# A transformer block in fp32 on one core: product 1 of a two-level Strassen scheme becomes a joint product too, and the sum it shares with products 6 and 7 is added to x by GpSimd

## The chip, the cores and the metric

The kernel runs on one core of a Trainium2 chip. The core has five engines with a queue of instructions each: TensorE (PE in the profile) multiplies matrices into PSUM, VectorE (DVE) and ScalarE (ACT) read PSUM and do elementwise work, GpSimd (POOL) does elementwise work on SBUF, and SyncE (SP) starts the DMAs. Each works its queue off in order; semaphores make an instruction wait for one of another engine. The metric is the device time of one execution in microseconds.

## The reference

x is 8 batches of 1024 rows of 1024 columns, fp32. Two steps follow each other, each added to x:

```python
x = x + xattn(layernorm(x), ctx, mask)        # 64 context rows a batch
x = x + ffn(layernorm(x), weight, lora_A, lora_B, router_w)

# xattn: softmax over the 64 unmasked rows of  h @ ctx.T / 32,  then  @ ctx
# ffn, h = layernorm(x):
base   = h @ weight.T                          # 1024 x 1024
probs  = softmax(h @ router_w.T)               # 8 experts; the top 2, weights made to sum to 1
Ax     = h @ lora_A.T                          # 8 experts x rank 16 = 128 columns
out    = base + 2 * sum over experts of  w_dense[e] * Ax[e] @ lora_B[e].T
```

## The kernel before, in words

**Pairs and rounds.** A tile has 128 rows of x; a pair has two tiles (r = 0, 1), 32 pairs in all (NP). `first()` (L896) takes the first two pairs and builds the weight sums. After it `quad(u)` (L1093) runs 15 times, for u = 2, 4, ..., 30: a round. It computes the ffn of the pairs u and v = u+1, and beside it the attention of the pairs behind them, called n, m, f and g (u+2 to u+5).

**The order is written out by hand.** All five engines run under `tc.manual_schedule` (L1307): every engine takes its instructions in the order in which the Python calls issue them. Semaphores come from the buffers: a write to a tile waits for its former readers. `hooks` are calls that `joint` makes at a given step, so that work of other pairs is issued between blocks of matmuls.

**The base product in two levels of Strassen's scheme (Winograd's form).** Level 1 halves the two tiles, the 1024 inputs and the 1024 outputs of a pair. That gives 7 products of 128x512 by 512x512, with sums of the operands: `has[u][:, 0]`, `has[u][:, 1]`, `hbs`, s1, s2, s4 (`rt_sums` L629 and `rt_sum_3` L640 form them on GpSimd), and of the weights: w11, w21, w22, t1 to t4. Product 8 here is the low-rank part of one quarter (`lora`, L694). Level 2 pairs the pairs u and v: `joint` (L788) does one product for both in 7 blocks of two 256-wide matmuls instead of 8. Its operand sums come from `joint_sums` (L774, four GpSimd operations), its weight sums q1 to q4 from `quarter_sums` (L680). Products 2 to 7 are joint. Product 1 is plain (`product`, L710): four 512-wide matmuls a pair, added to three quarters of x by `one_add` (L735) on VectorE. Each partial sum of a joint product goes from PSUM into x by VectorE (`to_x`, L806). Product 6 belongs to three quarters: it goes into the tile's own spent operand (`t_of`, L740), its first parts by ScalarE and VectorE copies, and GpSimd's `six_add` (L744) adds that to x. Product 7 belongs to two quarters and is added to x twice by VectorE.

**Routing.** `rt_low_rank_tile` (L572) multiplies a tile with the 128 low-rank columns and 8 router columns into `pa`, a PSUM tile of one bank (L574). ScalarE copies it to `axl`, a tile of one buffer (L582, L583). `rt_top` (L585) finds the two best experts on VectorE, with one exponential on ScalarE in the middle (L595), and scales `axl` in place (L612). `rt_turn_low_rank` (L614) transposes it on TensorE (`trw`, L621) and ScalarE copies the result to `axwt` (L623), which all `lora` matmuls read.

**Attention and norms.** `x_sums`, `x_squares` and `x_root` (L189 to L212) give the first norm on ScalarE; a pass over a tile is an ACTIVATE of 1024 columns. `att_scores` (`sct`), `att_sc` (`sc`), `att_shift`, `att_exp`, `att_divide`, `att_turn_p` (`ptp`), `att_readout` (`ro`) and `att_add` follow. `f_sums`, `f_squares`, `f_std`, `f_rows` give the second norm; its rows go to DRAM and come back blocked, and VectorE transposes them (`rt_turn_tile`). `att_turn_tile` does the same with x.

**PSUM.** Six banks (`ps_pp`) go round among chains, joint products (`jl`, `ju`), read-outs and the like; one bank each is kept for the attention and for the router.

**The start of a round (L1104 to L1224).** TensorE's order for u = 4 to 26: product 1 of u, the end of the joint product 4 before, the low-rank products of u, product 1 of v with `sc` inside, the low-rank products of v with `trw` of u between its tiles, product 8 of u, read-out of n, `ptp`, scores of f and g, read-out of m, then joint 6, 2, 7, 3, 5, 4. `rt_top(u)` is issued ahead of the second tile's x_sums and of x_squares.

Of the kernel before, what the change touches and what calls it, by code (L numbers as in the profile page):

```python
# [24 lines left out]
def kernel(  # L25
# [631 lines left out]
    quarters = {}  # L657
# [4 lines left out]
    def quarter_sums_steps(name: str, w):  # L662

        by = nc.gpsimd.tensor_tensor
        b11, b12, b21, b22 = [quarter(w, i, j) for i in (0, 1) for j in (0, 1)]
        q2, q3, q4 = [
            const.tile([P, HK, HH], F32, name=f"{name}_{i}") for i in (2, 3, 4)
        ]
        quarters[name] = b11, b21, b22, b12, q2, q3, q4

        def one():
            by(q3, b22, b12, ALU.subtract)

        def two():
            by(q2, q3, b11, ALU.add)
            by(q4, b21, q2, ALU.subtract)

        return one, two

    def quarter_sums(name: str, w):  # L680
        for do in quarter_sums_steps(name, w):
            do()

# [51 lines left out]
    def one_add(u: int, which=(0, 1, 2)):  # L735

        for i in which:
            add(u, pps[u][1], *((0, 0), (0, 1), (1, 0))[i])
# [5 lines left out]
    def six_add(u: int):  # L744
        for r, c in ((1, 0), (1, 1), (0, 1)):
            xc = xts[u][r][:, ts(c, HB)]
            nc.gpsimd.tensor_tensor(xc, xc, t_of(u), ALU.add)  # L747
# [3 lines left out]
    BOTH = {5: ((0, 1), (1, 1)), 7: ((1, 0), (1, 1))}  # L751
# [12 lines left out]
    def operand(i: int, p: int):  # L764
# [5 lines left out]
        return {3: sms[p][:, 1], 5: sms[p][:, 0], 7: has[p][:, 1]}[i]  # L770
# [17 lines left out]
    def joint(i: int, u: int, hooks, final: bool = False, aside: bool = False):  # L788
# [12 lines left out]
        name = {2: "w21", 3: "w22", 4: "t4", 5: "t1", 6: "t2", 7: "t3"}[i]  # L801
# [4 lines left out]
        def to_x(p, src, first: int, n: int):  # L806
            if i == 6:
                t = t_of(p)[:, first : first + n]
                if n == HH and (p == u and first == 0 or aside):
                    nc.scalar.copy(t, src)  # L810
                elif n == HH:
# [84 lines left out]
    def first():  # L896
# [153 lines left out]
        t1_two()  # L1050
        quarter_sum("t2")
# [7 lines left out]
        quarter_sums("w21", w21)  # L1059
        product_add(1, 7)  # L1060
# [15 lines left out]
        quarter_sums("w22", w22)  # L1076
        quarter_sum("w22")
        quarter_sum("w21")
        quarter_sums("t4", t4)
        att_scores(4)  # L1080

        def last():
            end()
            store(1, 1)
            quarter_sum("t4")
# [5 lines left out]
    pending = []  # L1091

    def quad(u: int):  # L1093
# [10 lines left out]
        product(u, 1, (lambda: att_sc(n)) if early else None, 1)  # L1104
# [4 lines left out]
        if new_mem:  # L1109
            mask_bias(b)  # L1110
        pending.pop()()
        if early:
            att_divide(n)
        one_add(u)
        rt_low_rank_tile(u, 0)
        if early:
            att_turn_p(n)
        rt_low_rank_tile(u, 1)
        if early:
            att_turn(m)  # L1120
        rt_turn_tile(v, 0)
        rt_top(u)
        rt_turn_tile(v, 1)
        if late:
# [4 lines left out]
            product(v, 1, lambda: att_sc(m))  # L1129
            if far:  # L1130
                att_turn_tile(f, 0)
                load_xs(g, (1,))
                att_turn_tile(f, 1)
            att_rstd(m)
            att_shift(m)
        rt_sum_3(u)
        rt_sums(v)
        if early:
            load_xs(f)
        elif far:  # L1140
            load_xt(f)
        if late:
            rt_low_rank_tile(v, 0)
            rt_turn_low_rank(u, bank_of(f"trw_{u}")[:, : 2 * P])
            att_exp(m)
            one_add(v, (0,))
        elif early:
            att_readout(n)
            att_scores(m)
            load_xs(g, (0,))  # L1150
            product(
                v, 1,
                {0: lambda: att_sc(m), 1: lambda: rt_turn_low_rank(u), 2: lambda: product(u, 8)},
            )
            att_rstd(m)
            att_exp(m)
            att_add(n)
            att_divide(m)
            f_sums(n)
# [3 lines left out]
            rt_low_rank_tile(v, 0)  # L1163
            att_turn_tile(f, 1)
        else:
            product(v, 1)
            rt_low_rank_tile(v, 0)
            rt_turn_low_rank(u, bank_of(f"trw_{u}")[:, : 2 * P])
        if far:
            att_turn_tile(g, 0)  # L1170
        if late:
            att_divide(m)
        if far:
            att_turn_tile(g, 1)
        if late and not far:
            att_readout(n)
            att_add(n)
        rt_low_rank_tile(v, 1)
        if early or late and not far:
            att_turn_p(m, True)  # L1180
        if not early:
            product(u, 8)
        joint_sums(6, u)
        rt_sum_3(v)
        if late and far:
            att_readout(n)
            att_turn_p(m, True)
        product_add(u, 8)
        if late and far:
# [6 lines left out]
        if far or not more:  # L1196
            rt_top(v)
        if more:
            att_readout(m)
        if late and not far:  # L1200
            att_add_tile(m, 0)
            rt_top(v)
        if late:
# [3 lines left out]
        if late and not far:  # L1207
            att_add_tile(m, 1)
        elif more:
            att_add(m)  # L1210
        left_over = []
        if late:
            one_add(v, (1,))
            left_over.append(lambda: one_add(v, (2,)))
        else:
            one_add(v)

        hooks = {5: left_over, 7: []}
        hooks[5 if more else 7].append(lambda: rt_turn_low_rank(v))
        if more:  # L1220
            hooks[2] = [lambda: f_squares(n), lambda: f_std(n)]
        if next_mem:
            hooks[5].append(lambda: turn_mem((f + 2) // PPB))
        end_6 = joint(6, u, hooks, aside=not more)  # L1224
        joint_sums(2, u)

        def low_v():
            product(v, 8)
            product_add(v, 8)

        def six():
            end_6()
            for p in (u, v):
                six_add(p)

# [119 lines left out]
```

## Time and profile before

| what | value |
| --- | --- |
| median of 3 runs | 1103.91 us (1103.2 to 1103.92) |
| span of the profiled execution | 1101.5 us |
| median less that span | 2.4 us |
| POOL, DVE, ACT busy in the span | 567.1, 819.8, 556.2 us |
| DMA moved | 174.01 MB, mean 158 GB/s |
| table loads of ACT, each | 1.28 us (four a round) |

The page gives the span, from the first to the last instruction; the time of a run holds a little more around it. An engine's busy time is the time in which its instructions ran. In the page's second part the span is cut in 40 slices; every slice but the first and the last has PE at 90% or more, and the granted clock at its full value. A timeline line is: start, length, engine, source line, operation, tile written <- tiles read, shape, number of records merged. An fp32 matmul leaves two records. What stands in brackets is the idle time before it and who ended it.

### The profile page before, as it was taken

How to read it: one execution, taken by the hardware profiler on the slowest of the kernel's cores; microseconds unless marked ns; L12 is line 12 of the kernel's file. 1: busy time of each engine (PE TensorE's matmuls, PEld its weight loads, DVE VectorE, ACT ScalarE, POOL GpSimd, SP SyncE). 2: the span in 40 equal slices, each digit the busy share in tenths (PEclk: the TensorE clock that was granted, in tenths of full speed). 3: DMA queues.
4: the chain of work that ended last, by engine and by line, in shares of the span. 5: the costliest groups of instructions: out<-in, count | busy, mean ns of one | idle time of the engine just before them, and what ended most of it. 6: DMA issues, size and time to landing. Idle time of an engine off the chain costs nothing.

```text
span 1101.5 us, 17562 instructions
## 1 busy us (share of the span) xinstructions
PE 1090.6 (99%) x5864; PEld 846.6 (77%) x5864; DVE 819.8 (74%) x2069; ACT 556.2 (50%) x1063; POOL 567.1 (51%) x629
## 2 busy tenths in 40 slices
PE   8999999999999999999999999999999999999998
PEld 6555787887878788787787878878787787877877
DVE  6666977769777687867869778687777778667665
ACT  4577363727539173573726638174472735636010
POOL 0079563635647265373644646356372644647372
PEclk9999999999999999999999999999999999999999
DMA  9857446363474625646265473635636355432301
GB/s 229 212 181 218 137 154 217 100 200 125 153 230 131 211 82 193 197 148 199 101 196 152 153 230 100 195 118 190 203 135 193 108 203 147 153 115 91 139 1 77
DMA packets 104921, 174.01 MB, mean 158 GB/s; under 512 B 12928, under 2 KB 77440, under 8 KB 104832
## 3 DMA queue, kind: packets, MB, share of 16 engines
q1 hardware_dynamic: 104832, 172.90, 50.3%
q8 instruction: 47, 0.77, 0.3%
q14 instruction: 42, 0.34, 0.1%
HBM read 107.84 MB, written 65.01 MB: 157 GB/s over the span
## 4 chain that ended last, share of the span: by engine, by line
PE 95%; DVE 2%; POOL 1%; ACT 1%; DMA 1%; SPq 0%; issue 0%; DVEq 0%; ACTq 0%; POOLq 0%
PE jl L703 28%; PE ju L703 21%; PE pa L578 10%; PE ch L703 9%; PE ro L480 5%; PE sct L412 5%; PE ju L695 4%; PE jl L695 3%; PE plain L703 3%; PE ch L695 2%; PE j L703 1%; DVE xT L89 1%; PE trw L621 1%; DMA xs<-in_x_dram 1%; PE ptp L466 1%; SPq L83 0%
## 5 line engine op out<-in xcount | busy, mean ns | idle before, releaser
L818 DVE TENSOR_TENSOR xt<-jl,xt 128x256 f32<-128x256 f32 x421 | 191.6, 485 | 139.6 <-PE jl L703 90.8
L818 DVE TENSOR_TENSOR xt<-ju,xt 128x256 f32<-128x256 f32 (+1 forms) x210 | 110.7, 551 | 56.2 <-PE ju L703 52.6
L635 POOL TENSOR_TENSOR s<-hA,hB 128x512 f32<-128x512 f32 x31 | 39.7, 1280 | 208.4 <-PE jl L703 92.9
L747 POOL TENSOR_TENSOR xt<-xt,hA 128x512 f32<-128x512 f32 x90 | 111.4, 1275 | 29.1 <-DVE hA L814 29.1
L195 ACT ACTIVATE junk<-xt 128x1024 uint8<-128x1024 f32 x60 | 63.2, 1053 | 123.6 <-DMA xt<-in_x_dram 123.1
L703 PE MATMUL ch<-w,hA 128*128 128x512 f32 x248 | 113.7, 593 | 0.0
L642 POOL TENSOR_TENSOR hA<-hA 128x512 f32<-128x512 f32 x31 | 39.6, 1277 | 139.8 <-PE pa L578 139.8
L703 PE MATMUL ju<-w,s_j 128*128 128x256 f32 x360 | 94.7, 385 | 0.2
L703 PE MATMUL ju<-t,s_j 128*128 128x256 f32 x360 | 92.7, 380 | 1.4 <-ACT hA L810 0.9
L692 DVE TENSOR_TENSOR xt<-ch,xt 128x512 f32<-128x512 f32 x124 | 81.3, 678 | 9.6 <-PE ch L703 4.5
L296 ACT ACTIVATE h<-xt,of_f 128x1024 f32<-128x1024 f32 x60 | 71.2, 1232 | 22.9 <-DVE of_f L292 14.1
L692 DVE TENSOR_TENSOR xt<-ro,xt 128x512 f32<-128x512 f32 x128 | 79.6, 676 | 3.7 <-PE ro L480 3.7
L703 PEld LDWEIGHTS ju<-t,s_j 128*128 128x128 f32 x360 | 66.2, 190 | 18.1 <-issue 5.3
L703 PEld LDWEIGHTS ch<-w,hA 128*128 128x128 f32 x248 | 44.7, 190 | 42.7 <-issue 41.8
L703 PE MATMUL jl<-t,s 128*128 128x256 f32 x300 | 76.0, 384 | 0.0
L703 PEld LDWEIGHTS ju<-w,s_j 128*128 128x128 f32 x360 | 63.9, 190 | 15.7 <-issue 6.8
L89 DVE STREAM_TRANSPOSE xT<-xs 128x1024 f32<-128x1024 f32 x60 | 73.6, 1229 | 0.6
L578 PEld LDWEIGHTS pa<-art_sb,hA 128*128 128x128 f32 x512 | 66.3, 190 | 9.8 <-issue 8.6
L578 PE MATMUL pa<-art_sb,hA 128*128 128x136 f32 x512 | 70.0, 280 | 0.0
L204 ACT ACTIVATE junk<-xt,of_x 128x1024 uint8<-128x1024 f32 x60 | 68.9, 1149 | 2.0
L578 PE MATMUL pa<-art_sb,hB 128*128 128x136 f32 x512 | 69.8, 279 | 0.0
L253 ACT ACTIVATE junk<-xt,of_f 128x1024 uint8<-128x1024 f32 x60 | 69.0, 1149 | 1.5
(202 smaller groups left out, 2425.0 us busy)
## 6 DMA issues: line engine op xcount, KB each, us to landing
xt<-in_x_dram SPq DMA_DIRECT2D x64, 512.0 KB, 4.8
out_dram<-xt SPq DMA_DIRECT2D x62, 512.0 KB, 3.0
xs<-in_x_dram SPq DMA_DIRECT2D x240, 128.0 KB, 4.1
hd<-h SPq DMA_DIRECT2D x60, 512.0 KB, 2.7
hs<-hd SPq DMA_DIRECT2D x240, 128.0 KB, 3.0
mem<-in_ctx_dram SPq DMA_DIRECT2D x16, 256.0 KB, 3.6
w<-in_w_t_dram SPq DMA_DIRECT2D x16, 256.0 KB, 10.0
ms<-in_ctx_dram SPq DMA_DIRECT2D x28, 64.0 KB, 2.0
```

The lines of the kernel that those rows point to most:

```text
L89: nc.vector.transpose(dst.rearrange("p k (t i) -> p t k i", i=NB), src.rearrange("p t (k i) -> p t k i", i=NB),)
L195: nc.scalar.activation(nowhere, xts[u][r], AF.Identity, accum_out=sm[:, r, :])
L204: nc.scalar.activation(nowhere, xts[u][r], AF.Square, bias=nm[:, r, :], accum_out=ss[:, r, :],)
L253: nc.scalar.activation(nowhere, xts[u][r], AF.Square, bias=nm[:, r, :], accum_out=ss[:, r, :])
L296: nc.scalar.activation(h, xts[u][r], AF.Identity, bias=nmr[:, r, :], scale=rstd[:, r, :])
L412: mm(sct[r * M : (r + 1) * M, :], mt[:, k, :], x_ts[u][r][:, k, :], start=(k == 0), stop=(k == KD - 1),)
L578: mm(pa[:, r, :], h, art_sb[:, k, :], start=(k == 0), stop=(k == KD - 1))
L692: tt(xc, bank, xc, ALU.add)
L695: mm(bank, axwts[u][:, r, :], lb_sb[:, c0 : c0 + n], start=alone, stop=True, skip_group_check=True)
L703: mm(bank, a[:, k, :], w[:, k, :], start=(start and k == 0), stop=(k == n - 1), skip_group_check=True)
L747: nc.gpsimd.tensor_tensor(xc, xc, t_of(u), ALU.add)
L818: tt(xc, src, xc, ALU.add)
```

## The change

Product 1 becomes joint for u and v, with weight sums of w11. `to_x` now gathers the products 1, 6 and 7 in one tile per pair: product 1 writes it (copies by ScalarE and VectorE), the products 6 and 7 add to it on VectorE. After each of the three, GpSimd's `t_add` adds the tile to the quarter of x whose sum is then complete: (0, 0) after product 1, (0, 1) after 6, (1, 1) and (1, 0) after 7. `one_add` and `six_add` go. Product 8 gets a bank of its own (`eight`, `eight_add`). There is no room for a further set of three weight sums, so those of t1 and w11 share `shared`: both are kept in DRAM and fetched once each a round. The sums of w22 and t4 are formed in the first round instead of `first()`. The joint products go 1, 2, 6, 3, 7, 5, 4. The start of a round is written anew: the low-rank products of u and v stand ahead of joint 1, `rt_top(u)` behind x_sums, x_squares and x_root of m, and the read-outs of n and m behind joint 1. The transposes of the next pair move from joint 3 and 5 into joint 4.

```diff
+    shared = const.tile([P, 3, HK, HH], F32, name="shared")
...
+        if name in ("t1", "w11"):
+            q2, q3, q4 = [shared[:, i] for i in range(3)]
+            kept[name] = dram.tile([P, 3, HK, HH], F32, tag=f"q_{name}", name=f"q_{name}", bufs=1)
...
+    def send_sums(name: str):
+        nc.sync.dma_start(out=kept[name], in_=shared)
+
+    def fetch_sums(name: str):
+        nc.sync.dma_start(out=shared, in_=kept[name])
...
+    def eight(u: int):
+        eights[u] = bank_of(f"eight_{u}")
+        lora(u, eights[u], 1, HB, HB, True)
+
+    def eight_add(u: int):
+        add(u, eights.pop(u), 1, 1)
...
+    def t_add(r: int, c: int, *pairs):
+
+        for p in pairs:
+            xc = xts[p][r][:, ts(c, HB)]
+            nc.gpsimd.tensor_tensor(xc, xc, t_of(p), ALU.add)
...
-            if i == 6:
+            if i in (1, 6, 7):
                 t = t_of(p)[:, first : first + n]
-                if n == HH and (p == u and first == 0 or aside):
+                if i == 1 and n == HH and (p == u and first == 0 or aside):
                     nc.scalar.copy(t, src)
-                elif n == HH:
+                elif i == 1 and n == HH:
                     nc.vector.tensor_copy(t, src)
                 else:
                     tt(t, src, t, ALU.add)
...
-        product(u, 1, (lambda: att_sc(n)) if early else None, 1)
         if late:
             x_sums(m, (0,) if far else (0, 1))
...
         pending.pop()()
+        rt_turn_tile(v, 0)
+        if not early:
+            rt_low_rank_tile(u, 0)
+        rt_turn_tile(v, 1)
+        rt_low_rank_tile(u, 1)
...
         if late:
             if far:
                 x_sums(m, (1,))
                 x_squares(m)
             x_root(m)
-            product(v, 1, lambda: att_sc(m))
...
+            att_sc(m)
+        rt_sums(v)
         rt_sum_3(u)
+        rt_top(u)
...
+        rt_low_rank_tile(v, 0)
+        if late and far:
+            att_turn_tile(f, 0)
+            load_xs(g, (1,))
+            att_turn_tile(f, 1)
...
+        rt_low_rank_tile(v, 1)
+        rt_sum_3(v)
+        joint_sums(1, u)
+        rt_turn_low_rank(u, bank_of(f"trw_{u}")[:, : 2 * P])
+        eight(u)
+        rt_top(v)
+        if late:
+            att_rstd(m)
+            att_shift(m)
+            if far:
+                att_turn_tile(g, 0)
...
+        end_1 = joint(1, u, hooks, aside=not more)
+        end_1()
+        joint_sums(2, u)
+        t_add(0, 0, u, v)
+        still_one()
+        eight_add(u)
...
+        if more:
+            att_divide(m)
+            att_readout(n)
+            att_turn_p(m, True)
...
+        rt_turn_low_rank(v, bank_of(f"trw_{v}")[:, : 2 * P])
+        eight(v)
+        eight_add(v)
...
+            if more:
+                fetch_sums("w11")
             if far:
                 load_xt(g)
...
-            hooks[3] = [lambda: rt_sums(n)]
+            hooks[3] = [lambda: rt_turn_tile(n, 0)]
+            hooks[5] = [lambda: rt_turn_tile(n, 1)]
+            hooks[7] = [lambda: rt_sums(n)]
```

fetch_sums("t1") stands in joint 6, after joint 1 is done with the place; in the last round it stands ahead of joint 6. `still_one` forms the w22 sums after joint 1 and the t4 sums after joint 2 of the first round, and nothing later.

## The prediction

> **What bounds the kernel now.** I read the busy rows first, then TensorE's waits, then one steady round (a round takes the pairs u and v = u+1) engine by engine. The page's first part:
>
> ```profile
> span 1101.5 us, 17562 instructions
> ...
> PE 1090.6 (99%) x5864; PEld 846.6 (77%) x5864; DVE 819.8 (74%) x2069; ACT 556.2 (50%) x1063; POOL 567.1 (51%) x629
> ```
>
> The list of who waited for whom, TensorE's part; these are among its longest in the whole run:
>
> ```profile
> PE ptp L466 <- ACT axl L583: 1.0, 2, 0.5
> PE ju L703 <- ACT hA L810: 0.9, 1, 0.9
> ```
>
> So TensorE (PE) sets the time and hardly ever waits: all its listed waits come to some 9 us of 1101.5. A change can win only by giving it less to do, and every new wait of PE is lost in full. The rounds start at 507.52 and 574.14: a period of 66.6 us. PE at the start of the second (start, length):
>
> ```profile
> 574.14 3.60 PE L703 MATMUL ch<-w,hA 128*128 128x512 f32 x8
> 577.58 0.59 PE L695 MATMUL jl<-lb_sb,axwt 128*128 128x256 f32 x2
> ...
> 581.72 1.02 PE L703 MATMUL ch<-w,hA 128*128 128x512 f32 x2
> 582.58 0.27 PE L426 MATMUL sc<-ident,scts 128*128 128x128 f32 x1
> 582.68 2.74 PE L703 MATMUL ch<-w,hA 128*128 128x512 f32 x6
> 585.26 1.09 PE L578 MATMUL pa<-art_sb,hA 128*128 128x136 f32 x8
> 586.19 1.09 PE L578 MATMUL pa<-art_sb,hB 128*128 128x136 f32 x8
> 587.12 0.38 PE L621 MATMUL trw<-ident,axl 128*128 128x128 f32 x2
> ```
>
> The starts count; the lengths overlap. The plain product 1 (`ch`) stands between u's low-rank product (four `pa` groups, 578.01 to 581.72, 3.71 us) and v's. ScalarE (ACT) meanwhile:
>
> ```profile
> 581.92 0.39 ACT L583 COPY axl<-pa 128x272 f32<-128x272 f32 x1 [5.94 <-PE pa L578]
> 582.80 0.20 ACT L595 ACTIVATE of_top<-of_top 128x2 f32<-128x2 f32 x1 [0.50 <-DVE of_top L594]
> 582.91 1.04 ACT L195 ACTIVATE junk<-xt 128x1024 uint8<-128x1024 f32 x1
> ...
> 586.85 1.28 ACT L212 ACT_TABLE_LOAD   x1
> 588.14 0.30 ACT L212 ACTIVATE of_x<-of_x,eps_sb 128x2 f32<-128x2 f32 x1
> 588.34 0.35 ACT L623 COPY axwt<-trw 128x256 f32<-128x256 f32 x1
> 588.71 1.28 ACT L448 ACT_TABLE_LOAD   x1
> ```
>
> The router's exponential (L595) goes ahead of the sums, squares and root of x (L195 to L212). That order is what the change breaks.
>
> **What it takes off PE.** Plain product 1 of a pair costs 577.58 - 574.14 = 3.44 us (four 512-wide matmuls; the second, less 0.1 for `sc`, the same): 6.87 a round. A joint product is seven blocks; a block starts 0.865 after the one before (574.14 - 573.28 = 0.86): 6.06. Product 8 stays two 512-wide matmuls. Gain 0.81 us a round, 12.2 in 15 rounds.
>
> **What it adds, one steady round (u = 4 to 26, 12 of them).** t counts from the end of joint 4 (574.14 before), T from the end of ACT's copy of `pa` to `axl` for u.
>
> (a) The low-rank products of u and v now stand together, with only `sc` (0.1) between, and `pa` has one bank. So v's first matmul waits for the copy. PE met that wait once: the `ptp` wait of 0.48 at 125.40, 0.64 after the `pa` before should have ended. Less `sc`: **0.53**. T is at t = 0.43 (end_4) + 3.71 + 0.59 = 4.7.
>
> (b) rt_top(u) is now written after x_sums(m, (1,)), x_squares(m) and x_root(m), and ACT runs in order: copy of `axl`, sums, squares, load, root, a second load, and only then the exponential. From the rows: 582.91 to 588.34 is 5.43, with the load before the next use 1.28 and the exponential 0.20: T+6.9. VectorE (DVE) then does L604 to L612, 583.47 to 584.97, 1.5: `axl` is ready at T+8.5. PE wants it (L621) after v's low-rank product, T+0.06+3.71. Today 5.4 us pass on PE between the two (581.72 to 587.12) and the exponential is first in line; now it waits **4.73**. Behind it in PE's queue stand eight(u) and all of joint 1, and everything waits for those.
>
> (c) `axl` has one buffer (line 582), so the copy of v's `axl` waits for PE's transposes of u's, and the copy to `axwt` comes behind that: transposes 0.22, release 0.2, copies 0.38 and 0.35: eight(u), directly behind, waits about 1.05. Then DVE: after rt_top(u), two transposes of 1.23, rt_top(v) 2.52 (595.93 to 598.45), att_rstd and att_shift 0.94, another transpose 1.2, and only then joint 1's copies out of PSUM, at T+15.7. PE wants the first of them done for its sixth block at T+15.0 (8.5+0.22+1.05+0.86, five blocks) and gets it at T+16.1. Joint 1 ends at T+17.9 instead of 8.5+0.22+0.86+6.06 = 15.6: **2.22** for both. POOL's sums for joint 1 (after rt_sum_3(v), four of 0.73 with gaps, done about T+9.4) are earlier than that, so POOL costs nothing here; without this cover it would be about 0.5.
>
> (d) After joint 1, DVE runs its last copy, two adds of 0.6 and eight_add(u) before it frees the bank of the fourth read-out of n: PE is there at 1.44, the bank at 2.42: 0.97. `ptp` waits for att_divide behind it: 0.1. eight(v) again follows its own transpose, with f_sums done in time: 0.64. **1.71**.
>
> (e) Joint 5 leaves DVE about 3.3 us late in joint 4, where a transpose of 1.3 now stands before a partial sum that PE waits for: about **0.15**.
>
> Sum 9.34 - 0.81 = 8.53; times 12 = **102.4**. The rest: u = 2 has no squares ahead, but shift, three transposes and divide (5.2 us of DVE) before `ptp`, of which PE covers 1: 4.2, with (a) and the two copies +6. u = 28 has sums and squares of both tiles (5.2 us of ACT) ahead of the copy of `axl`, which comes some 3 us late, then root and second load, 0.9 past PE, and (c), (d) without half their DVE work, 4: with the gain off +7. u = 30 has none of it, only the copies: about +0.5. Together 116.
>
> Costed at nothing: product 7's one target and one_add's removal (DVE 74% busy, no PE wait ends on it before); t_add and joint 1's sums (+5.5 us of POOL a round, busy 34.6 of 66.4); the w22 and t4 sums in round 2 (POOL sat idle 7.1 there). Each is about 1 us a round if that cover is gone, which is why the range stays open above.
>
> Unknown prices. First, the two fetches of 768 KB. The w11 fetch goes onto SP ahead of load_xt(g); x's first tile lands at t = 0.7 today. At 308 GB/s (570 to 575) a fetch is 2.5 us, at 222 3.5; ACT's first x_sums then ends at t = 4.4 to 5.4 and the copy of `axl` wants ACT at 4.3: 0 to 1 us a round; I take 0.1, since the queue was fullest there. The fetched weights have 15 us or more until use, and a 512 KB load lands in 4.8. Second, TensorE's clock after a gap of 5 us. Gaps of 1 us cost nothing here (the read-outs after 14.29 take 1.92 as later). But the first eight 128-wide matmuls of the run take 3.64 (0.455 each), three at 12.43 some 0.26 each. If the gap does that for 5.5 us, joint 1 ends 1.25 later (the rest hides in DVE's wait). 0 to 15 us in all; I take 4, nearer the gaps' row.
>
> [...]
>
> **The sum.** The profiled execution spans 1101.5 and the median of the runs is 1103.9; the 2.4 lies around the span. 1103.9 + 116 + 5 = **1225 us**.
>
> **Rivals.**
> 1. Only what ACT's order and the copies force stays (a, b and the two waits of 0.64), and the DVE and bank waits of (c), (d) melt because DVE has 4 us a round less to do: 0.53 + 4.73 + 1.28 - 0.81 = 5.7, times 12, plus 9: **1181**. For it: one_add goes. Against it: those adds stood before other work than this.
> 2. The gap also halves the clock and the fetch delays x: + 1.25 + 0.9 a round on all of it: **1251**.
> 3. The other side: not slower. The mechanism is ACT being ahead of PE at L621: if exponential and copies are through by T+2.2, PE never waits and keeps the 12.2: **1092**. It decides as soon as less than 2.2 us of ACT work stands between the copy of `axl` and the exponential. The order of the changed program puts 6.7 there, so it needs my reading of ACT's queue to be wrong.
> 4. The change does not bring its product: shared weights land late and PE waits at joint 1's first block. It needs a fetch of over 15 us: over 1270.
>
> **How the numbers follow.** Forecast (1200 to 1245) 0.52; rival 1 (1150 to 1200) 0.20; rival 2 (1245 to 1270) 0.17; rival 4 0.04; rival 3 0.04; in between 0.03. The range reaches from rival 1 to rival 2 with its bounds: 1180 to 1258. A measurement here can tell 0.2% from no change: faster 0.04, same 0.01, slower 0.95.
>
> **What would show it.** TensorE's waits: L621 for DVE's `axl` (L612), about 57 us in 12; `pa` for ACT's `axl`, about 7; `eight` for ACT's `axwt`, 15 to 25; joint 1's `ju` for DVE's copies, 12 or more; `ro` for DVE's adds, about 12. In ACT's timeline the exponential behind two table loads. PE's share near 88%, its busy time about 12 lower, the period about 75 us. The forecast is wrong if the exponential stands ahead of the squares, if L621 waits under 3 us, or if the granted clock falls below 1.

## The result and the profile after

The changed kernel takes **1281.77 us** (median of 4 runs, 1281.21 to 1284.03) against 1103.91 (1103.2 to 1104.57): a ratio of 1.1615, 95% interval 1.1598 to 1.1631. That is 178 us more. The forecast was 1225, its range ended at 1258: the direction was right, the size was not. The profiled execution spans 1280.3 us.

The page of the changed kernel, first part and clock row:

```profile
span 1280.3 us, 18061 instructions
...
PE 1142.9 (89%) x6044; PEld 898.5 (70%) x6044; DVE 831.7 (65%) x1979; ACT 557.7 (44%) x1063; POOL 655.6 (51%) x723
...
PEclk9998898999989999898998989989899898999999
```

TensorE's share fell from 99% to 89%, and two things stand here that were not in the kernel before: a granted clock below full speed in some slices, and a PE busy time that grew by 52 us although the change takes work away. The list of what TensorE waited for (us in total, times, longest us):

```profile
PE trw L621 <- DVE axl L612: 75.6, 23, 5.6
PE eight L706 <- ACT axwt L623: 23.6, 30, 1.0
PE ptp L466 <- DVE s L457: 15.6, 16, 5.7
PE pa L578 <- ACT axl L583: 7.8, 14, 2.7
PE jl L706 <- DVE xt L834: 7.2, 14, 0.5
```

Those five come to 130 us; in the kernel before the whole list comes to 7.3 (the prediction read it as some 9). A steady round takes 78.5 us instead of 66.5 (from the first L621 of u = 4 to that of u = 26, over 11 rounds). Here is one of them, the stretch behind u's low-rank product (start, length):

```profile
669.72 0.39 ACT L583 COPY axl<-pa 128x272 f32<-128x272 f32 x1 [1.89 <-PE pa L578]
...
671.35 1.27 POOL L635 TENSOR_TENSOR s<-hA,hB 128x512 f32<-128x512 f32 x1 [3.19 <-DVE top L591]
671.36 1.28 DVE L594 TENSOR_TENSOR of_top<-top 128x2 f32<-128x2 f32 x1
...
672.96 1.04 DVE L599 CAST of_top<-idx 128x4 f32<-128x4 uint32 x1
...
676.86 0.20 ACT L595 ACTIVATE of_top<-of_top 128x2 f32<-128x2 f32 x1
677.10 0.71 DVE L604 TENSOR_SCALAR of_top<-of_top 128x2 f32<-128x2 f32 x1 [1.72 <-ACT of_top L595]
...
679.34 1.02 DVE L612 TENSOR_TENSOR axl<-axl,we 128x128 f32<-128x128 f32 x2
...
679.69 0.47 PE L621 MATMUL trw<-ident,axl 128*128 128x128 f32 x1 [5.55 <-DVE axl L612]
...
681.64 2.08 PE L706 MATMUL eight<-lb_sb,axwt 128*128 128x512 f32 x2 [0.75 <-ACT axwt L623]
```

The exponential stands 6.9 us behind the copy of `axl`, as forecast. What the forecast did not have: VectorE's subtraction of two columns (L594) takes 1.28 us, its conversion of four (L599) 1.04, L604 0.71, the two multiplications of L612 1.02. In the kernel before these take 0.16, 0.17, 0.16 and 0.49, and GpSimd is idle beside them:

```profile
582.61 0.16 DVE L594 TENSOR_TENSOR of_top<-top 128x2 f32<-128x2 f32 x1
...
583.08 0.17 DVE L599 CAST of_top<-idx 128x4 f32<-128x4 uint32 x1
...
583.47 0.16 DVE L604 TENSOR_SCALAR of_top<-of_top 128x2 f32<-128x2 f32 x1
...
584.48 0.49 DVE L612 TENSOR_TENSOR axl<-axl,we 128x128 f32<-128x128 f32 x2
...
586.26 1.28 POOL L635 TENSOR_TENSOR s<-hA,hB 128x512 f32<-128x512 f32 x1 [3.95 <-DVE hB L89]
```

In the changed kernel GpSimd's additions (L635 on) start 10 ns before L594 and go on to 680.96. And `eight`, which for v in the same round (at 700.53) takes 1.13, takes 2.08. The next lines are three stretches of that round: start and end, length, busy time (and instructions) of PE, PEld, DVE, ACT and POOL, granted clock, share of the DMA engines, GB/s:

```profile
673.90:679.60 5.70, 0.24 (x3) 0.03 (x1) 3.81 (x11) 3.11 (x5) 5.46 (x7) 0.89 1.01 345
679.60:685.20 5.60, 4.50 (x9) 2.57 (x10) 5.25 (x22) 0.86 (x3) 1.35 (x2) 0.51 0.29 105
685.20:690.50 5.30, 5.30 (x25) 4.19 (x23) 3.02 (x8) 1.04 (x5) 1.45 (x2) 1.00 0.00 0
```

TensorE idles for 5.5 us and then runs 5.6 us at half speed (granted clock 0.51). The trace has 17 stretches at half speed, of 3.3 to 6.8 us, 109 us in all; the kernel before has one, of 1.1 us, behind its last instruction.

### The profile page after: what moved, and what is told of

Same layout as the page of the kernel before. It is cut to its first block, busy times and chain, and to the rows that moved or that the text cites. A ratio compares the mean times of both kernels' runs of the same rounds, so it can differ in the third digit from the quotient of the medians.

```text
span 1280.3 us, 18061 instructions
## 1 busy us (share of the span) xinstructions
PE 1142.9 (89%) x6044; PEld 898.5 (70%) x6044; DVE 831.7 (65%) x1979; ACT 557.7 (44%) x1063; POOL 655.6 (51%) x723
## 4 chain that ended last, share of the span: by engine, by line
PE 71%; DVE 10%; ACT 9%; DMA 6%; issue 2%; POOL 1%; SPq 1%; DVEq 0%; ACTq 0%
PE jl L714 28%; PE ju L714 20%; PE sct L412 5%; PE eight L706 4%; PE pa L578 3%; DMA xs<-in_x_dram 3%; PE jl L706 3%; PE ju L706 3%; ACT junk L243 2%; PE plain L714 2%; ACT junk L204 2%; DVE xt L834 2%; DMA xt<-in_x_dram 2%; DMA out_dram<-xt 1%; DVE hA L830 1%
## 5 line engine op out<-in xcount | busy, mean ns | idle before, releaser
L834 DVE TENSOR_TENSOR xt<-jl,xt 128x256 f32<-128x256 f32 (+1 forms) x301 | 140.1, 485 | 131.0 <-PE jl L714 107.1
L763 POOL TENSOR_TENSOR xt<-xt,hA 128x512 f32<-128x512 f32 x120 | 150.7, 1283 | 101.6 <-DVE hA L830 96.3
L798 POOL TENSOR_TENSOR s_j<-s 128x256 f32<-128x256 f32 x45 | 32.9, 730 | 203.2 <-PE jl L714 173.2
L714 PE MATMUL ju<-w,s_j 128*128 128x256 f32 x480 | 124.9, 383 | 0.1
L635 POOL TENSOR_TENSOR s<-hA,hB 128x512 f32<-128x512 f32 x31 | 39.7, 1279 | 145.9 <-DVE hB L89 69.0
L834 DVE TENSOR_TENSOR xt<-ju,xt 128x256 f32<-128x256 f32 (+1 forms) x150 | 79.6, 547 | 42.7 <-PE ju L714 33.3
L830 DVE TENSOR_TENSOR hA<-jl,hA 128x256 f32<-128x256 f32 (+1 forms) x135 | 68.8, 510 | 55.6 <-PE jl L714 55.2
L714 PEld LDWEIGHTS ju<-w,s_j 128*128 128x128 f32 x480 | 86.6, 189 | 18.6 <-issue 2.6
L703 DVE TENSOR_TENSOR xt<-ro,xt 128x512 f32<-128x512 f32 x128 | 80.4, 675 | 29.6 <-PE ro L480 29.6
L798 POOL TENSOR_TENSOR s_j<-hB 128x256 f32<-128x256 f32 x30 | 21.8, 726 | 132.3 <-PE jl L714 132.3
L621 PE MATMUL trw<-ident,axl 128*128 128x128 f32 x64 | 19.4, 370 | 75.6 <-DVE axl L612 75.6
L621 PEld LDWEIGHTS trw<-ident,axl 128*128 128x128 f32 x64 | 9.0, 159 | 92.4 <-DVE axl L612 80.8
L830 DVE TENSOR_TENSOR hA<-ju,hA 128x512 f32<-128x512 f32 (+1 forms) x75 | 43.3, 578 | 41.8 <-PE ju L714 36.1
```

Of the source, the lines that this page charges most:

```text
L703: tt(xc, bank, xc, ALU.add)
L714: mm(bank, a[:, k, :], w[:, k, :], start=(start and k == 0), stop=(k == n - 1), skip_group_check=True)
L763: nc.gpsimd.tensor_tensor(xc, xc, t_of(p), ALU.add)
L830: tt(t, src, t, ALU.add)
L834: tt(xc, src, xc, ALU.add)
```

## The experiments

Theory: three things together make the loss, ScalarE's order (the exponential behind the squares and root), VectorE's small operations held up beside GpSimd's additions, and half speed of TensorE after the wait. Rivals: the order alone; VectorE's queue or GpSimd's sums alone; the slow clock as something that costs nothing. "A round" is again the mean from u = 4 to u = 26, and the idle time at L621 is the mean before the first transposition of u in the same rounds.

| kernel | us | a round | mean idle time at L621 | at half speed |
|---|---|---|---|---|
| before | 1103.9 | 66.5 | none | 1 us |
| changed | 1281.8 | 78.5 | 5.4 | 109 |
| e1 exponential first | 1258.2 | 76.8 | 3.7 | 82 |
| e2 filled wait | 1279.9 | 78.5 | 1.1 | 51 |
| e3 GpSimd held back | 1323.9 | 82.1 | 4.2 | 121 |
| e4 waits ahead removed | 1286.1 | 78.8 | 6.9 | 136 |
| e5 before, exponential late | 1175.9 | 72.1 | 3.6 | 50 |
| e9 as e5, wait filled | 1162.0 | 71.2 | 1.0 | 3 |
| e6 = e1 and e3 | 1257.0 | 77.1 | none | 51 |
| e11 as e6, copies first | 1271.2 | 77.5 | none | 76 |
| e7 rework | 1207.6 | 72.7 | none | 46 |
| e8 joint 6 second | 1212.1 | 73.6 | none | 20 |
| e10 as e8, waits moved | 1227.2 | 75.1 | none | 78 |
| e12 as e10, other banks | 1189.3 | 72.0 | none | 36 |

e3 has one run, the others four.

**e5: ScalarE's order alone, in the kernel before.**

```diff
-        rt_top(u)
+        if not late:
+            rt_top(u)
         rt_turn_tile(v, 1)
...
             x_root(m)
+            rt_top(u)
```

> The kernel before, with one part of the change alone: rt_top(u) written behind x_sums(m, (1,)), x_squares and x_root, in the rounds u = 4 to 28. Plain products, weights and GpSimd's sums stay as they are. Theory (the order on ScalarE alone makes a wait at L621, also with the plain product 1 of v as cover): axl comes 8.5 to 9 us after its copy instead of 2.6, TensorE wants it 4.8 us after, so it waits 3.7 to 4.2 us a round, 0.5 to 1.3 more if the gap halves its clock: 4 to 5.5 a round over 13 rounds, 1155 to 1175 us. Rival (the order matters only where the cover is gone, as in the changed kernel): within 5 us of 1104.

Measured: 1175.9 us (ratio 1.0654, 1.0636 to 1.0671), 1 us above the theory's range. From its list of waits:

```profile
PE trw L621 <- DVE axl L612: 46.0, 14, 3.7
```

The order is a cause by itself, worth 72 us even with the plain product 1 as cover. A round grew by 5.6: 3.65 at L621, and most of the rest because the matmuls around its end run at half speed for 3.41 us (6.83 in two rounds).

**e9: the same with the wait filled.** In the rounds u = 4 to 28, 12 matmuls of `ident` by `ident` go into the bank of `trw` ahead of its transposes and are overwritten.

```diff
+        if fill:
+            for _ in range(12):
+                mm(bank[:, :P], ident, ident, start=True, stop=True)
         for r in range(2):
             nc.tensor.transpose(trw[:, r, :], axl[:, r, :ER], ident)
```

> The kernel before with rt_top(u) written behind x_squares and x_root, as in the run e5 (1175.9 us, wait of 3.65 at L621 and a half-speed stretch of 3.4 us behind it in nearly every round), and 12 matmuls of ident by ident (128 wide, 2.8 us in all) put into the bank of trw ahead of its transposes, so that TensorE is idle for under 1 us there. axl comes no earlier by this. Theory (idle time of some 3.5 us halves the clock for 3.4 us, which costs 1.7 us a round by itself): the stretches go and the time falls by 12 to 13 times 1.5 to 1.8: 1152 to 1158 us. Rival (the slow stretch is free, or does not come from idle time): 1172 to 1178 us. In the changed kernel the same filler was worth 2 us in all (e2), since joint 1 then waited for GpSimd's sums; here there are none.

Measured: 1162.0 us, 14 less than e5; the half-speed stretches are gone but one at the end. So work put into an idle time, useless as it is, makes the kernel faster: the idle time itself had cost speed. It was 1.0 a round and not 1.5 to 1.8, so the time lies 4 us above the theory's range; one wait came up in its place:

```profile
PE ptp L466 <- DVE s L457: 8.6, 13, 1.0
```

**e1: the order undone in the changed kernel.**

```diff
         if late:
+            rt_top(u)
             if far:
                 x_sums(m, (1,))
...
         rt_sums(v)
         rt_sum_3(u)
-        rt_top(u)
+        if not late:
+            rt_top(u)
```

> The changed kernel, with rt_top(u) written ahead of x_sums(m, (1,)), x_squares and x_root, so that ScalarE has the router's exponential directly behind the copy of axl, as in the kernel before. Theory 1 (ScalarE's order makes the gap at L621, VectorE's small operations slowed beside GpSimd's sums lengthen it, and the gap halves TensorE's clock): the wait at L621 falls from 5.7 us a round to 2.0 to 3.5, held up by the slowed operations alone; the gap is then too short for the clock, which stays at full speed and gives 2.1 us more: 4.3 to 5.8 a round over 13 rounds, 1206 to 1226 us. Theory 2 (the order alone, as the prediction priced it, with no slowing by GpSimd): the wait at L621 is 0 to 0.3, 1180 to 1200 us. Rival (the order is not the cause, VectorE's queue is): no change, 1282 us.

Measured: 1258.2 us, 24 less, where theory 1 had 56 to 76: outside every range. Theory 2 falls, since it had no wait at L621. Theory 1 had the clock wrong: that a wait of 2.0 to 3.5 us would leave it at full speed was its author's estimate, and each steady round still has a half-speed stretch, of 6.83 us behind the waits of 4.7 and of 3.41 behind those of 2.7. The exponential is through 0.7 and 2.8 us behind the copy of `axl`, in turn, and still L621 waits 2.7 and 4.7 us in turn. One round:

```profile
660.60 1.28 DVE L594 TENSOR_TENSOR of_top<-top 128x2 f32<-128x2 f32 x1
...
662.20 1.04 DVE L599 CAST of_top<-idx 128x4 f32<-128x4 uint32 x1
...
667.79 1.03 DVE L612 TENSOR_TENSOR axl<-axl,we 128x128 f32<-128x128 f32 x2
...
668.14 0.48 PE L621 MATMUL trw<-ident,axl 128*128 128x128 f32 x1 [4.75 <-DVE axl L612]
```

`rt_top` takes 7.3 to 8.4 us from its first instruction to its last, against 2.6 in the kernel before: it now lies in GpSimd's 9.6 us of additions with its whole length, where in the changed kernel its middle was spent waiting for ScalarE anyway. The second cause was hidden behind the first, and e3 and e6 below show that it is about as strong.

**e3: GpSimd held back.** A two-column addition on GpSimd reads `axl` behind `rt_top(u)`; `rt_sums(v)` and `rt_sum_3(u)` are queued behind it.

```diff
+        rt_top(u)
+        gate(u)
         rt_sums(v)
         rt_sum_3(u)
-        rt_top(u)
```

> The changed kernel, with a tiny GpSimd addition that reads axl behind rt_top(u), and rt_sums(v), rt_sum_3(u) behind it in GpSimd's queue, so that GpSimd rests while VectorE does rt_top(u). Its sums for joint 1 thereby come late, so the whole time says little; the durations are what is looked at. Theory (the tail of rt_top(u) is slowed by GpSimd's additions): L594, L599, L603, L604, L606, L608, L609 fall back to 0.16 to 0.18 us each and L612 to 0.29; the wait at L621 falls from 5.7 to about 4.7 in steady rounds; rt_top(2) takes 2.6 us instead of 7.7. Joint 1 then waits some 2.5 us for its sums: 1285 to 1320 us. Rival (these operations are slow for another reason, such as the table loads or ScalarE's reads): their durations stay at 0.4 to 1.3 us.

Measured: 1323.9 us in one run, 4 above the range; the durations fell as the theory said, and the wait at L621 to 4.3:

```profile
687.44 0.16 DVE L597 TENSOR_TENSOR of_top<-top 128x2 f32<-128x2 f32 x1
...
687.92 0.17 DVE L602 CAST of_top<-idx 128x4 f32<-128x4 uint32 x1
...
692.96 0.20 ACT L598 ACTIVATE of_top<-of_top 128x2 f32<-128x2 f32 x1
...
694.56 0.68 PE L628 MATMUL trw<-ident,axl 128*128 128x128 f32 x2 [4.33 <-DVE axl L615]
```

(L597 and L602 are L594 and L599 of the changed kernel.) With GpSimd still, `axl` is ready 8.5 us behind its copy, as the prediction had it, and rt_top(2) takes 2.6 us instead of 7.8. The prediction's step (b) was right for a VectorE that is left alone. The price of the gate, sums that come late for joint 1, is larger than the gain; in its list stands

```profile
PE jl L721 <- ACT hA L833: 24.1, 15, 1.7
```

a copy that waits for GpSimd (see e11).

**e6: both undone.** The edits of e1 and e3 together.

> The changed kernel, with rt_top(u) ahead of x_sums(m, (1,)), x_squares and x_root, and GpSimd held back by a tiny addition that reads axl until rt_top(u) is through. Theory (two causes each strong enough to hold L621: ScalarE's order, and VectorE's small operations beside GpSimd's sums; only both undone free it): rt_top(u) takes 2.6 us as in the kernel before, TensorE waits under 0.4 us at L621, and there is no half-speed stretch behind it. What is saved (5.5 and 2 us a round) comes back in part: the sums for joint 1 end about 13 us after the copy of axl, 2 us after joint 1 wants them, and rt_top(v) now lies beside them and is slowed to some 6 us, which delays VectorE's copies for joint 1. Net 2 to 6 us a round over 13 rounds and 5 in round 2: 1200 to 1250 us. Rival (GpSimd's sums are the real bound of this stage, and hiding rt_top(u) gains nothing): 1265 to 1290 us.

Measured: 1257.0 us (ratio 1.1397, 1.1354 to 1.1441), just above the theory's range, below the rival's. The wait at L621 is gone in every round. The four runs show both causes apart, by the time from the copy of `axl` until it is scaled (in the steady rounds): with both 9.3 to 10.3 us, with the order alone (e3) 8.5 to 8.8, with GpSimd alone (e1) 7.4 and 9.5, with neither 2.7 and 3.6. Either one is enough to hold L621. What stands at the head of the list instead is the next link:

```profile
PE eight L713 <- ACT axwt L630: 49.7, 30, 3.4
```

ScalarE has the squares and the root of x ahead of the copy of `axwt`, so the order that held up the exponential now holds up `eight`, by 3.4 and 2.5 us.

**e11: those copies first too.**

```diff
-                x_squares(m)
-            x_root(m)
...
         eight(u)
         rt_top(v)
+        if late:
+            if far:
+                x_squares(m)
+            x_root(m)
```

> The run e6 (1257 us; exponential first, GpSimd gated; its wait had moved from L621 to eight, 3.4 and 2.5 us in turn, for ScalarE's copy of axwt behind the squares and root of x), with x_squares and x_root moved behind the copies of axl of v and axwt of u. Theory (the stalls form a chain: ScalarE's order, then GpSimd's sums of 9.6 us behind the gate, then VectorE's rt_top(v) beside those sums, each hiding the next): the wait at eight falls to 0.8, and 1 to 2 of the 2.5 us gained come back inside joint 1, which waits for copies into hA behind GpSimd's sums: 1225 to 1245 us. Rival (ScalarE's order is all that is left in e6): 2.2 us or more a round over 13 rounds, 1215 to 1228 us. Second rival (nothing gained, GpSimd's sums set joint 1's end alone): 1252 to 1260 us.

Measured: 1271.2 us, slower than e6, outside all three ranges. `eight` waits 0.8 as forecast, but joint 1 gives more than that back, two lines of its list:

```profile
PE ju L721 <- POOL s_j L805: 24.0, 14, 2.3
...
PE jl L721 <- ACT hA L833: 22.3, 15, 1.7
```

The second is GpSimd too: joint 1 leaves its sum in its own operand `hA`, and ScalarE may not write there before `joint_sums(1)` has read it. Behind the gate GpSimd's sums set joint 1's end, and half-speed stretches return with these waits (76 us of them against 51 in e6).

**e2: the wait filled in the changed kernel.** As e9, with 20 matmuls.

> The changed kernel, with 20 matmuls of ident by ident (128 wide, some 0.22 to 0.25 us each, about 4.6 us in all) put into the bank of trw ahead of its transposes, in the rounds u = 4 to 28; their result is overwritten. They fill most of TensorE's wait at L621 and depend on nothing new. Theory (the half-speed stretches of 6.8 us come from TensorE's being idle in that wait, and cost some 2 us a round): the granted clock reads 1.0 in these rounds, eight takes 0.86 and not 1.87, a round is 1.5 to 2.2 us shorter over 13 rounds: 1253 to 1263 us. Rival (the slow stretch is a limit on power or contention that follows the sums, not idleness): the stretches stay, 1280 to 1288 us. Second rival (the clock costs nothing, since joint 1 would wait for VectorE or GpSimd at full speed instead): clock 1.0, but 1278 to 1283 us.

Measured: 1279.9 us, 1.9 less than the changed kernel, no more than its own runs differ by. The time is that of the second rival, but the clock is not: seven of the twelve steady rounds still have a slow stretch. In the other five `eight` runs at full speed (1.13 us) and a round takes 77.6 on average instead of 78.5; in each of these joint 1 is then 1.0 us too early for its sums:

```profile
PE ju L717 <- POOL s_j L801: 5.8, 6, 1.0
```

Some rounds have a longer wait of `ptp`. So of the 2 us a round that half speed takes from the changed kernel, 0.9 came back where the clock stayed up; what a full clock in every round would bring is not shown.

**e4: the waits ahead of L621 removed.** u's first low-rank half ahead of end_4, and `pa` of v in a bank of its own.

```diff
+        if not early:
+            rt_low_rank_tile(u, 0)
         pending.pop()()
         rt_turn_tile(v, 0)
-        if not early:
-            rt_low_rank_tile(u, 0)
...
-        rt_low_rank_tile(v, 0)
+        rt_low_rank_tile(v, 0, apart=True)
```

> The changed kernel, with the first half of u's low-rank product put ahead of end_4, as cover for the wait of its lora for VectorE, and with pa of v in a bank of its own. Theory: the wait of jl at L706 (0.67 a round) goes and brings axl forward by as much; the wait for pa (0.53) goes too, but comes back at L621, where TensorE waits for VectorE in any case. So 0.5 to 0.7 us a round over 14 rounds: 1271 to 1275 us. Rival (the waits add up as they are listed): 1.2 a round, 1263 to 1266 us. Second rival (both are hidden behind the wait at L621, because ScalarE's x_sums sets when axl is copied): 1280 to 1284 us.

Measured: 1286.1 us, 2 above the second rival's range. Both waits went from the list, 15 us together, and more than that came back at L621:

```profile
PE trw L624 <- DVE axl L615: 99.9, 20, 7.9
```

In the round shown above, TensorE is at L621 8.9 us after the end of joint 4 instead of 9.5, and goes on at 15.0 instead of 15.1. GpSimd's additions start when VectorE has turned v, 6.7 us after that end in both.

**e7, e8, e10, e12: product 1 joint, the waits taken away one by one.** e7 has e1 and e3; u's first low-rank half ahead of end_4; read-out of n and scores of f between the low-rank products and L621; rt_top(v) behind joint 1; eight(u) inside joint 1, eight(v) inside joint 2.

```diff
+        rt_low_rank_tile(u, 0)
         pending.pop()()
...
+        rt_top(u)
+        gate(u)
...
+            att_readout(n)
...
+        if late:
+            att_add(n)
...
+            att_scores(f, True)
         rt_turn_low_rank(u, bank_of(f"trw_{u}")[:, : 2 * P])
-        eight(u)
-        rt_top(v)
...
+            hooks[5] = [lambda: eight(u)]
         end_1 = joint(1, u, hooks, aside=not more)
...
+            rt_top(v)
...
+        hooks = {1: [lambda: eight(v)], 2: [lambda: eight_add(v)], 5: []}
         end_2 = joint(2, u, hooks)
```

> The changed kernel with product 1 joint and the waits taken away one by one: rt_top(u) first on ScalarE and GpSimd gated behind it; u's low-rank product ahead of end_4; read-out of n and scores of f as cover between the low-rank products and the transposes of axl; rt_top(v) moved behind joint 1's copies; eight(u) inside joint 1 and eight(v) inside joint 2, so that they no longer wait for axwt. If the account of the stalls is complete, what is left a round is some 1 us at joint 1 for GpSimd's sums, 0.5 in joint 4, and little else: 67 to 69.5 us a round against 66.5 of the kernel before and 78.5 of the changed one; rounds 2 and 30 keep some of theirs: 1120 to 1160 us. Rival (the waits are shifted, not removed, since VectorE and GpSimd have no room in this stage): over 1190 us. Below 1104 only if the gain of 0.8 us a round on TensorE survives, which needs under 0.3 us of wait a round.

Measured: 1207.6 us, 72.7 a round: 74 us of the 178 regained, but 3 a round more than the range, and the time is the rival's. What is left in its list:

```profile
PE jl L721 <- ACT hA L833: 20.2, 15, 1.7
PE ro L480 <- ACT s L471: 16.0, 13, 1.3
```

e8 takes joint 6 second, with rt_top(v) inside it, scores of g and eight(u) inside joint 1, and the read-out of m behind joint 6.

```diff
+            hooks[3].append(lambda: att_scores(g, "rt"))
+            hooks[4] = [lambda: eight(u)]
         end_1 = joint(1, u, hooks, aside=not more)
...
+            hooks[6].append(lambda: rt_top(v))
+        end_6 = joint(6, u, hooks)
+        if more:
+            att_turn_p(m, True)
+        end_6()
...
             att_readout(m)
...
         end_2 = joint(2, u, hooks)
```

> The run e7 carried on (product 1 joint, order first on ScalarE, GpSimd gated), against what e7 still waited for (jl for ScalarE's copy behind GpSimd's sums 1.56, the transposed p and the read-out of m 2.3, scores for VectorE's transposes 0.85, half clock 1.7 a round): rt_turn(v) ahead of end_4, the transposes of axl ahead of the scores, scores of f ahead of joint 1 and those of g and eight(u) inside it as cover for GpSimd's sums, joint 6 (which needs no axwt) second, rt_top(v) inside it, and the read-out of m behind it. If the account holds: 66.0 to 68 us a round against 72.5 in e7 and 66.5 in the kernel before; round 2 some 5 us shorter than in e7, since its division comes before three transposes: 1100 to 1135 us. Rival (the joint product 1 needs more of GpSimd and VectorE in this stage than the stage has): over 1160 us.

Measured: 1212.1 us, 73.6 a round: the rival. The waits of e7 went or were halved; new ones came up, 2.0 a round in joint 2 for VectorE, whose step there waits for a root late on ScalarE, and 1.3 for the transposes of x.

e10 goes on from e8; it also moves the load of f's x behind the transposes of g:

```diff
-        elif far:
-            load_xt(f)
...
-            att_scores(f, True)
+            load_xt(f)
...
+                hooks[2] = [lambda: att_scores(f, True)]
...
-            att_turn_p(m, True)
+            hooks[6].append(lambda: att_turn_p(m, True))
...
-        rt_turn_low_rank(v, bank_of(f"trw_{v}")[:, : 2 * P])
+        rt_turn_low_rank(v)
...
+            f_std(n)
             x_stats(f)
```

> The run e8 carried on (waits of one of its rounds: 0.8 at the scores of f, 0.4 to 1.0 at the read-out of m, 0.6 to 0.9 at v's transposes, 1.4 to 2.6 in joint 2 for VectorE's step that stands behind ScalarE's late f_std): scores of f two blocks into joint 1, p transposed before joint 6's last block, v's transposes in another bank, f_std ahead of x_stats. If the named waits are all there is: 3 to 4.5 us a round less than the 73 of e8, 68.5 to 70, and 1155 to 1175 us in all. Rival (each wait taken away uncovers another on VectorE or GpSimd): 1195 to 1215 us. It would be faster than the kernel before only with rounds under 66.5, which this does not reach by either.

Measured: 1227.2 us, worse, above both ranges. The scores of f stood two blocks into joint 1 in a bank that its third block needs, and ScalarE copied them out only behind its copy into `hA`, which waits for GpSimd, 4.3 and 3.6 us in turn:

```profile
PE ju L723 <- ACT scts L419: 47.2, 12, 4.3
```

e12 undoes that point:

```diff
-                hooks[2] = [lambda: att_scores(f, True)]
-                hooks[3].append(lambda: att_scores(g, "rt"))
+                hooks[3].append(lambda: att_scores(f, "rt"))
+                hooks[3].append(lambda: att_scores(g, True))
```

> The run e10 (1227 us) put right in one point: there the scores of f stood in the bank that joint 1's upper half wants, and ScalarE copied them out only behind a copy that waits for GpSimd's sums, so joint 1's third block waited 4.3 and 3.6 us, with a half-speed stretch behind it. Here the scores of f and g both follow joint 1's third block, f in the bank of pa. If that was all: the even rounds of e10, 74.1 us, less 4.3, 1.0 and 3.4 for the clock, 65 to 66, plus what comes up in its place, at least 1 us: 66.5 to 69 a round, 1125 to 1160 us in all, still above the kernel before, since rounds 2 and 30 keep some 17 us. Rival (as before, the next wait on VectorE, ScalarE or GpSimd takes its place): 71 or more a round, over 1185 us.

Measured: 1189.3 us (ratio 1.0787, 1.0737 to 1.0838), the best with product 1 joint, and again the rival: 72.0 a round. Undisturbed rounds take 70.0 to 70.4; the others wait again, for data:

```profile
PE sct L414 <- DVE xt L712: 28.0, 12, 3.4
```

The read-out's addition that this line names stands on VectorE behind a transpose of x, and those wait 49 us for the loads of xs in all; in e8 it is already 47.5 us, in e7 2.8. In a round of 70.0, at full clock, TensorE is busy for 67.2 us and idle for 2.8; in the kernel before it is busy for all of its 66.6. So the 0.81 that the forecast took off a round does not show as less busy time even there. No kernel with product 1 joint came near 1103.9.

## Why the prediction was wrong, by its own steps

**What was right.** TensorE bounds the kernel and every wait is lost (99% to 89%). The gain on TensorE can only be small: joint 1's blocks start 0.86 apart at full speed (the 0.81 itself shows in no round). **(a)** 0.53: measured 0.53. **(b)** on ScalarE: exponential at T+6.9, measured T+6.9; the tail of 1.5 is what e3 shows. **(d)** at the read-out and `ptp`: 1.07, measured 1.06, though by luck: 0.54 of it is the wait of `ptp` for VectorE's division, priced at 0.1, and the read-outs lost the rest, priced at 0.97. The fetches cost nothing: 768 KB land in 5.4 and 5.5 us, and no wait names `shared`. Rival 4's time (over 1270) came true without its mechanism. Of rival 2 the clock came true; x came late but no wait of TensorE names it. A granted clock below 1 was one of the three signs that the prediction named of being wrong.

**Where it failed.** The total missed by 57 us.

- **(b) "VectorE then does L604 to L612 ... 1.5"**, and with it u = 2 and u = 30. The duration was taken from rows beside which GpSimd stood still (its next addition begins at 586.26, the tail is over at 584.97), and the change puts 9.6 us of GpSimd work just there. The edit was costed at nothing since VectorE and GpSimd were far from full; the price was not room but that these operations of VectorE take longer beside GpSimd's (L604 0.71 us for 0.16, L612 1.02 for 0.49). Measured: the tail takes 3.26 for 1.5 in the round shown, and TensorE is held at L621 for 5.72 instead of 4.73, counted from the end of v's low-rank product; rt_top(2) 7.8 for 2.6, part of why u = 2 lost 18.5 and not 6; rt_top(30) 7.3 for 3.0, where u = 30 lost 6.5 and not 0.5. u = 2 lost 4.3 at L621, where nothing was priced, and 1.9 and 5.7 at `ptp`, where 4.2 was priced. The trace of the kernel before could have warned: in its last round GpSimd works beside the second `rt_top`, and that one takes 5.9 us instead of 2.6:

```profile
1055.51 0.49 DVE L599 CAST of_top<-idx 128x4 f32<-128x4 uint32 x1
...
1057.44 1.32 DVE L608 TENSOR_TENSOR we<-we,of_top 128x16 f32<-128x16 f32 x2
1057.46 1.26 POOL L642 TENSOR_TENSOR hA<-hA 128x512 f32<-128x512 f32 x1
```

- **The clock, "0 to 15 us in all; I take 4"**, and the price of 1.25 a round in rival 2. Each steady round has a stretch at half speed; in the example it takes 2.1 us of (c). It is part of why (c) measured 3.59 (from L621's start to joint 1's end, 10.73, less 7.14) for 2.22. The other part of (c) was wrong in kind: VectorE's copies came in time, 688.04 and 688.91, since TensorE came later. "Gaps of 1 us cost nothing" was the nearest row in length of gap, but 5 us lay outside what the trace could say, whose longest wait of TensorE is 1.6; e5 shows that 3.65 is enough, e1 that 2.7 can be.
- **A step that was not priced:** end_4's `lora`, which loses its cover when product 1 of u leaves, 0.67 a round. (d)'s eight(v) was 1.02 for 0.64, (e) some 0.3 for 0.15.

Steady rounds: 12.0 instead of 8.5, so 41 of the miss; u = 2 12.5, u = 28 2.8, u = 30 6; less the 5 allowed.

**The sum itself.** As a tally of idle times it holds: about 13 a round, less the gain, is the 12 measured. As a list of what could be won back it does not. e4 removed 1.2 a round and won nothing, e2 kept the clock up in five more rounds and won 2 us in all, e1 removed the order and won 24 of the 72 that the same order costs in the kernel before. The waits lie behind one another: ScalarE's order, VectorE beside GpSimd, GpSimd's sums for joint 1; removing one uncovers the next.

Over the whole changed kernel, these operations of VectorE, which have two SBUF inputs, are slower on average when GpSimd works beside them: L594 (0.74 us for 0.16), L603 (0.71 for 0.17), L606 (0.52 for 0.16), L609 (0.55 for 0.17) and L612 (0.55 for 0.29). A conversion and a TENSOR_SCALAR with one input are slowed too (L599 1.02 for 0.17, L604 0.45 for 0.16). The half-speed stretches, but for those that a run's end cuts short, are 3.41, 6.83 or (in e4) 10.24 us long: 3.41 once, twice or three times.

Open: why e2 has some rounds of 80 us, why the loads of xs come late from e8 on, what else e12's round of 70.0 does for longer than a round before, what slows VectorE beside GpSimd, what sets the length of the slow stretches, and how much of 178 each cause holds. They overlap, so no split adds up.

## What to carry to other kernels

A duration from a profile holds only beside what ran beside it: when a change puts GpSimd work next to small VectorE operations such as these, price them at what they took there (L594 0.16 us with GpSimd still and up to 1.28 beside GpSimd's additions of 1.28; in e1 a chain of 2.6 us grew to between 7.3 and 8.4). When TensorE gets a wait like those measured here, count with a slow stretch after it: 93 of 94 waits of 3.1 us or more had one, and 30 of 61 of 1.8 to 3.1. And before dissolving a wait, look for what is late directly behind it: here one stall hid another (e1 alone left a wait of 3.7 us at L621, e3 alone 4.2, both together none), so a single edit told too little and a pair was needed.

## What the runs showed that was not expected

- **VectorE beside GpSimd.** Over the whole changed kernel, the conversion of 128x4 (L599) takes 0.17 us when GpSimd is still (17 times) and 1.02 when it works (15 times); the subtraction of 128x2 (L594) 0.16 and 0.74. Not slowed there are RECIPROCAL (L605, 0.17 in both), MAX8 and FIND_INDEX8 (0.16) and additions that read PSUM (L703, 0.68 and 0.67). The averages hide a range: L594 takes from 0.16 to 1.28 beside GpSimd. GpSimd's own additions of 512 columns take 1.26 to 1.28 on average beside these operations and 1.26 to 1.30 otherwise, so VectorE pays nearly all; beside L612, in half the rounds, one of GpSimd's short sums takes 0.86 instead of 0.73.
- **Half speed after short waits.** In the changed kernel and the twelve experiments, 93 of the 94 waits of TensorE of 3.1 us or more have a half-speed stretch that begins in them or within 3.6 us behind them; of the waits of 2.4 to 3.1 us it is 21 of 37, of those of 1.8 to 2.4 us 9 of 24 (waits in the first 60 us and the last 8 left out). In e5 a wait of 3.65 us is followed by a stretch of 3.41 or 6.83 us in 11 of 12 rounds. In e7 two waits of 0.97 and 1.30 within 2.6 us were followed by one too, so not only a single long gap does it.
- **Useless work can pay.** 2.8 us a round of matmuls without a use made e5 faster by 14 us.
